# A fixed VectorE order over two row blocks, output terms per step, and a hinted branch in a top-p attention loop

## The chip, the cores and the metric

The kernel runs on one core of one Trainium2 chip. The metric is the device time of one execution in microseconds; lower is better. Each run is repeated, and each study run is timed beside runs of the kernel before on the same chip.

Names: PE is TensorE, PEld its weight load, DVE is VectorE, ACT is ScalarE, POOL is GpSimd. "L589" is line 589 of that kernel's own file, so the same work has different line numbers in different kernels. The granted clock is the share of its full speed at which PE was let run, as the trace recorded it. A branch hint is an instruction that marks a branch as likely to be taken.

## The reference

A graph attention layer over 4096 nodes with 256 features makes `x1`. A second layer takes the layer norm and a relu of it, spreads it over the graph, and does two steps of top-p attention. Only the second layer's attention matters here:

```python
def _top_p_attention(X, W1, W2, W3):
    q = X @ W1.T @ W2.T
    k = X @ W3.T
    logits = q @ k.T / TAU
    probs = jax.nn.softmax(logits, axis=-1)
    idx = jnp.argsort(-probs, axis=-1)
    sp = jnp.take_along_axis(probs, idx, axis=-1)
    cs = jnp.cumsum(sp, axis=-1)
    keep_sorted = cs - sp < TOP_P
    ...  # mask: keep_sorted, back in the order of the columns
    A = probs * mask
    return A / jnp.maximum(A.sum(-1, keepdims=True), 1e-12)
...
for n in range(STEPS):
    A = _top_p_attention(Xa, W1, W2, W3)
    Xf = R @ Xf
    Xa = A @ Xa
    Z = Z + Xf @ U1[n].T + Xa @ U2[n].T
h = X + Z
...  # layer norm of h, times ln_g, plus ln_b; the caller adds x1
```

The attention matrix of 4096 x 4096 is worked in 32 row blocks of 128 rows, in each of the two steps.

## The kernel before

A block passes through these pieces. The threshold of each row is found without sorting: three probes, each of which sums the entries under a guess, then the largest 48 entries under the last guess are sorted.

```python
def second_probe(r):                 # DVE 128x4096, then some 20 small POOL operations give the third guess c3
    nc.vector.scalar_tensor_tensor(big, r.e, r.c2, r.e, ALU.is_le, ALU.mult, accum_out=L)
    ...
def candidates(r):                   # DVE: third probe, maxima of 16 segments, sort, threshold r.t, flags
    nc.vector.scalar_tensor_tensor(big, r.e, r.c3, r.e, ALU.is_le, ALU.mult, accum_out=L)
    ...
    nc.vector.tensor_scalar(flags[:, 1:], after, r.t, flags[:, :1], ALU.is_equal, ALU.max)
    r.count = ps2.tile([P, 512], F32, name="mm")
    nc.tensor.matmul(r.count[:1, :2], ones[:, :1], flags, start=True, stop=True)   # PE counts the flagged rows

def masked(r):
    nc.vector.tensor_copy(cnt, r.count[:1, :2])
    with tc.If(nc.values_load(cnt[:, 1:], **dve) > 0, ...):    # rare: ties, or the threshold not among the 48
        with tc.If(nc.values_load(cnt[:, :1], **dve) > 0):
            searched(r.e, r.z, r.t, big)                       # bisection, over 31 probes: a long piece of program
        untied(r.e, r.z, r.t, big)
    nc.vector.scalar_tensor_tensor(r.e, r.e, r.t, r.e, ALU.is_ge, ALU.mult, accum_out=kept)   # "the mask"
    nc.vector.reciprocal(scale, kept)

def attend(e, scale, cur, dst):      # PE: 8 groups of four transposes and four accumulations; ACT copies between
    ...
def finish(b, xa2):                  # step two only: four output terms on PE, then the layer norm on DVE
    ...

for b in range(NB):
    r = begun.pop(b)
    if b + 2 < NB:
        begun[b + 2] = first_probe(kT, qT, nm, sg, c1, b + 2)   # PE logits, ACT exponentials and sign passes
    candidates(r)
    if b + 1 < NB:
        second_probe(begun[b + 1])
    if b + 2 < NB:
        first_step(begun[b + 2])                                # POOL: second guess c2
    scale = masked(r)
    attend(r.e, scale, cur, xa)
    if n == 0:
        nc.scalar.dma_start(xa_d[b], xa)
    else:
        finish(b, xa)
```

The order of instructions on each engine is set ahead of time by a scheduler that works from program order and estimates; only the dependencies are the programmer's.

## Time and profile before

| | before |
|---|---|
| time, median of 3 runs | 4451.24 us (4449.61 to 4453.26) |
| span of the profiled run | 4455.6 us |
| mask to mask, step one (mean of 31 intervals) | 31.79 us |
| mask to mask, step two | 41.47 us |
| last mask of step one to first of step two | 179.0 us |

The time from the start of one block's mask to that of the next is the measure used throughout: the two loops are 62 such intervals, and what is saved in one is saved 31 times. The prediction shows the lines of this profile.

### The profile page before, as it was taken

Reading aid. Unit: us, or ns where it says so; the run is one execution under the profiler, and the core shown is the slowest. Engines: PE = TensorE matmul, PEld = TensorE weight load, DVE = VectorE, ACT = ScalarE, POOL = GpSimd, SP = SyncE. Lnnn points to the kernel's source line nnn. Section 1 sums busy time; section 2 is a strip of 40 time slices with the busy share of each in tenths; the row PEclk is TensorE's granted clock in tenths of the full one; section 3 lists DMA queues with packets and bytes.
Section 4 is the critical chain, followed back from the end, with each engine's and each line's share of the span. In section 5 each row is a group of like instructions: output and inputs, shape, how many; then the busy total and the mean of one; then the engine's idle time right before and its main releaser. Section 6 shows DMA issues by size and latency. Waiting matters only on the chain. (4 is left out here: it accounts for less than half of the span.)

```text
span 4455.6 us, 55548 instructions
## 1 busy us (share of the span) xinstructions
PE 3426.5 (77%) x19239; PEld 2653.2 (60%) x19239; DVE 2882.5 (65%) x5564; ACT 2161.2 (49%) x4250; POOL 1391.9 (31%) x2857
## 2 busy tenths in 40 slices
PE   3598786879459999758888888885677787787787
PEld 1287786868337777526565655663555565555465
DVE  4587887888535544248686877742756667667565
ACT  2476665757211100356665656536344545544543
POOL 2100000000110000136566565613445454445453
PEclk7599898989659999868888888896788788888888
DMA  7416152440238888100000000010000000000000
GB/s 167 152 68 144 60 129 97 106 115 35 83 108 273 276 282 271 61 2 5 6 4 6 5 5 6 5 43 1 10 15 10 15 13 13 15 15 10 15 13 10
DMA packets 175128, 297.34 MB, mean 67 GB/s; under 512 B 15008, under 2 KB 82592, under 8 KB 174752
## 3 DMA queue, kind: packets, MB, share of 16 engines
q1 hardware_dynamic: 114160, 224.30, 15.4%
q0 software_dynamic: 16896, 33.56, 4.3%
q10 hardware_dynamic: 43696, 35.15, 2.4%
q8 instruction: 154, 2.52, 0.2%
q14 instruction: 222, 1.82, 0.1%
HBM read 292.62 MB, written 33.88 MB: 73 GB/s over the span
## 5 line engine op out<-in xcount | busy, mean ns | idle before, releaser
L641 PE MATMUL acc<-X,eT 128*128 128x256 f32 x4096 | 1014.3, 403 | 18.9 <-ACT eT L638 11.7
L641 PEld LDWEIGHTS acc<-X,eT 128*128 128x128 f32 x4096 | 809.4, 203 | 198.6 <-ACT eT L638 87.2
L228 PE MATMUL acc<-ut,m 128*128 128x195 bf16 (+1 forms) x8192 | 761.9, 255 | 174.6 <-DVE m L222 111.7
L228 PEld LDWEIGHTS <-m 128*128 128x128 bf16 x8192 | 730.0, 100 | 206.6 <-DVE m L222 103.0
L219 ACT ACTIVATE g<-sr,d_c 128x1024 bf16<-128x1024 f32 x512 | 560.4, 1153 | 291.0 <-DVE m L223 267.3
L638 ACT COPY eT<-tp 128x512 f32<-128x512 f32 x512 | 283.5, 587 | 832.1 <-PE tp L636 831.6
L636 PE MATMUL tp<-ident,e 128*128 128x128 f32 x2048 | 344.6, 325 | 378.2 <-DVE e L590 378.2
L301 PE MATMUL racc<-hl,ar 128*128 128x512 f32 x2048 | 515.0, 409 | 148.5 <-DVE hl L284 75.0
L636 PEld LDWEIGHTS tp<-ident,e 128*128 128x128 f32 x2048 | 301.9, 170 | 424.3 <-issue 393.4
L301 PEld LDWEIGHTS racc<-hl,ar 128*128 128x128 f32 x2048 | 391.5, 196 | 271.7 <-DVE hl L284 92.3
L342 PE MATMUL mm<-kT,qT 64*128 64x512 f32 x1024 | 468.1, 719 | 98.0 <-ACT e L461 82.9
L506 POOL TENSOR_TENSOR sums<-sums 128x8 f32<-128x8 f32 (+1 forms) x128 | 215.6, 1684 | 787.9 <-ACT void L498 782.9
L461 ACT ACTIVATE e<-mm,nm 128x512 f32<-128x512 f32 x512 | 346.2, 684 | 183.1 <-PE mm L342 166.5
L590 DVE SCALAR_TENSOR_TENSOR e<-e,t 128x4096 f32<-128x4096 f32 x64 | 287.0, 4484 | 164.1 <-issue 112.5
L222 DVE TENSOR_TENSOR m<-g,ax 128x2048 bf16<-128x2048 bf16 x256 | 313.1, 1223 | 76.5 <-issue 54.8
L342 PEld LDWEIGHTS mm<-kT,qT 64*128 64x128 f32 x1024 | 150.7, 205 | 320.8 <-ACT e L461 254.0
L554 DVE MAX8 cand<-big 128x8 f32<-128x256 f32 x1024 | 340.8, 410 | 0.1
L519 DVE SCALAR_TENSOR_TENSOR big<-e,lowered 128x4096 f32<-128x4096 f32 x64 | 286.9, 4483 | 60.8 <-POOL lowered L476 60.7
L547 DVE SCALAR_TENSOR_TENSOR big<-e,lowered 128x4096 f32<-128x4096 f32 x64 | 286.7, 4480 | 38.1 <-POOL lowered L476 38.1
L223 DVE TENSOR_TENSOR m<-g,ax 128x2048 bf16<-128x2048 bf16 x256 | 311.2, 1216 | 0.0
L496 ACT ACTIVATE void<-e,c 128x1024 uint8<-128x1024 f32 x256 | 293.3, 1146 | 2.2
L297 DVE CAST ar<-at 128x1024 fp32r<-128x1024 f32 x256 | 176.1, 691 | 181.0 <-DMA at<-in_adj_t_dram 149.5
(195 smaller groups left out, 3852.3 us busy)
## 6 DMA issues: line engine op xcount, KB each, us to landing
at<-in_adj_t_dram SPq DMA_DIRECT2D x256, 512.0 KB, 4.7
ut<-uv_d SPq DMA_DIRECT2D x64, 784.0 KB, 7.0
ax<-in_adj_t_dram POOLq DMA_DIRECT2D x32, 1024.0 KB, 9.5
uv_d<-parts ACTq DMA_DIRECT2D x128, 98.0 KB, 1.9
xb<-in_x_dram SPq DMA_DIRECT2D x64, 128.0 KB, 2.1
sr<-s_d SPq DMA_DIRECT2D x16, 512.0 KB, 3.7
x<-x_d SPq DMA_DIRECT2D x64, 128.0 KB, 2.3
xf_d<-xf ACTq DMA_DIRECT2D x64, 128.0 KB, 4.0
```

What stands on the lines that cost most here:

```text
L219: nc.scalar.activation(g[:, c, :], sr, AF.Sign, bias=d_c[:, h, j0 + c:j0 + c + 1])
L222: nc.vector.tensor_tensor(m[0], g, a, ALU.is_equal)
L223: nc.vector.tensor_tensor(m[1], g, a, ALU.is_lt)
L228: nc.tensor.matmul(acc[i][:, t, :cols], m[t][:, c, ts(i, P)], ut[:, j, t, :cols], start=(j == 0 and t == 0), stop=(j == NB - 1 and t == 1))
L301: nc.tensor.matmul(acc[i].rearrange("p s d -> p (s d)"), ar[:, c, ts(i, P)], hl[hop][:, j].rearrange("p s d -> p (s d)"), start=(j == 0), ...
L342: nc.tensor.matmul(pm, qT[ts(c % 2, DA), ts(b, P)], kT[ts(c % 2, DA), ts(c // 2, 512)], start=True, stop=True)
L461: nc.scalar.activation(e[:, ds(c % 2 * N // 2 + c // 2 * 512, 512)], pm, AF.Exp, bias=nm[:, b:b + 1], accum_out=sums[:, c // 2, c % 2:c % ...
L496: nc.scalar.activation(void, r.e[:, ts(q, N // 4)], AF.Relu, bias=r.c1, scale=-1.0, accum_out=sums[:, q, 2:3])
L554: nc.vector.max(cand[:, s, :], big[:, ts(s, N // SEG)])
L590: nc.vector.scalar_tensor_tensor(r.e, r.e, r.t, r.e, ALU.is_ge, ALU.mult, accum_out=kept)
L636: nc.tensor.transpose(pt[:, i, :], e[:, ts(4 * g + i, P)], ident)
L641: nc.tensor.matmul(acc, eT[:, i, :], cur[:, j, :], start=(j == 0), stop=(j == NB - 1))
```

## The change

The intent is to keep VectorE busy across the two waits of a block. VectorE's order is fixed by hand over two row blocks, so that the third probe of block b+1 lies between the flags of block b and the use of their count. The output terms are multiplied in each step right after the attention, and what VectorE has to do with them ("closing": an addition in step one, the layer norm in step two) comes one block later, ahead of the next mask. The rare branch is turned round and hinted. First probes run three blocks ahead instead of two.

```diff
-    ps2 = ctx.enter_context(tc.tile_pool(name="ps2b", bufs=3, space=PSUM))
+    ps2 = ctx.enter_context(tc.tile_pool(name="ps2b", bufs=2, space=PSUM))
-    l1e = ctx.enter_context(tc.tile_pool(name="l1e", bufs=4))
+    l1e = ctx.enter_context(tc.tile_pool(name="l1e", bufs=5))
 ... (logits tiles of two banks; ScalarE pieces twice as wide; fewer GpSimd operations)
     def second_probe(r):
         L = col("L")
-        nc.vector.scalar_tensor_tensor(big, r.e, r.c2, r.e, ALU.is_le, ALU.mult, accum_out=L)
+        nc.vector.scalar_tensor_tensor(junk, r.e, r.c2, r.e, ALU.is_le, ALU.mult, accum_out=L)
 ...
+    def third_probe(r):                       # was the head of candidates(r)
+        r.L = col("L3")
+        nc.vector.scalar_tensor_tensor(big, r.e, r.c3, r.e, ALU.is_le, ALU.mult, accum_out=r.L)
 ...
-    def masked(r):
+    def masked(r, label):
         cnt = small.tile([1, 2], I32, name="cnt", bufs=2)
         nc.vector.tensor_copy(cnt, r.count[:1, :2])
-        with tc.If(nc.values_load(cnt[:, 1:], **dve) > 0, preferred_fallthrough_block=False):
-            with tc.If(nc.values_load(cnt[:, :1], **dve) > 0):
-                searched(r.e, r.z, r.t, big)
-            untied(r.e, r.z, r.t, big)
+        with tc.If(nc.values_load(cnt[:, 1:], **dve) == 0, label=label, preferred_fallthrough_block=False) as none:
+            pass
+        with none.Else():
+            with tc.If(nc.values_load(cnt[:, :1], **dve) > 0):
+                searched(r.e, r.z, r.t, junk)
+            untied(r.e, r.z, r.t, junk)
 ...
-    def finish(b, xa2):
-        ... (four parts transposed and multiplied here, then the layer norm, for step two alone)
+    def contribute(n, r, xf, xa):
+        parts = [transposed(rows, ps2, t, f"zT{i}") for i, t in enumerate((xf, xa))]
+        for i, t in enumerate(parts):
+            for k in range(KC):
+                nc.tensor.matmul(r.acc[:, 1, :], t[:, k, :], u_s[2 * n + i][:, k, :], start=(i == 0 and k == 0),
+                                 stop=(i == len(parts) - 1 and k == KC - 1))
+
+    def finish(n, b, r):
+        if n + 1 < STEPS:
+            nc.vector.tensor_add(r.part, r.acc[:, 1, :], X[:, b, :])
+            nc.sync.dma_start(z_d[b], r.part)
+        else:
+            nc.gpsimd.tensor_tensor(r.x1, r.x1, ln_b_r, ALU.add)
+            hb = rows.tile([P, D], F32, name="hb", bufs=1)
+            nc.vector.tensor_add(hb, r.acc[:, 1, :], r.part)
+            normalized(hb, hb)
+            nc.vector.tensor_mul(hb, hb, ln_g_r)
+            nc.vector.tensor_add(hb, hb, r.x1)
+            nc.sync.dma_start(out[ts(b, P), :], hb)
 ...
-        for b in range(NB):
-            ... (the loop shown above)
+        with tc.manual_schedule(engines={ET.DVE}):
+            second_probe(begun[0])
+            third_probe(begun[0])
+            last = None
+            for b in range(NB):
+                r = begun.pop(b)
+                label = f"usual{n}_{b}"
+                tc.mark_branch_hint_location(label, "LikelyTaken", engines=[ET.DVE])
+                if b + 1 < NB:
+                    second_probe(begun[b + 1])
+                candidates(r)
+                if b + 1 < NB:
+                    third_probe(begun[b + 1])
+                if b + 2 < NB:
+                    first_step(begun[b + 2])
+                if last:
+                    finish(n, b - 1, last)
+                masked(r, label)
+                pair = attend(n, b, r, cur)
+                if b + 3 < NB:
+                    begun[b + 3] = first_probe(kT, qT, nm, sg, c1, b + 3)
+                contribute(n, r, *pair)
+                last = r
+            finish(n, NB - 1, last)
```

## The prediction

> **What bounds the kernel now.** I read the page first: 4455.6 us, and no engine above 77%, so no engine's sum sets the time. Then busy time by stage, to find the stretches that the change touches: the attention loop runs from 1965 us to the end, in two steps of 32 row blocks. In both, PE (about 0.82 busy), DVE (0.75 and 0.67) and ACT leave gaps at once, so the loop is bound by a chain that goes from engine to engine. The columns are stretch, length, PE, PEld, DVE, ACT, POOL busy, PE clock, DMA share, GB/s:
> ```profile
> 2350.00:2550.00 200.00, 165.06 (x689) 118.28 (x689) 149.66 (x321) 124.07 (x258) 117.59 (x228) 0.87 0.02 5
> 2226.20:2230.60 4.40, 0.00 (x0) 0.00 (x0) 4.40 (x3) 3.35 (x6) 0.97 (x1) 0.50 0.00 2
> 3700.00:4000.00 300.00, 241.59 (x1031) 174.25 (x1029) 199.64 (x474) 149.64 (x331) 140.40 (x315) 0.84 0.05 14
> ```
> The list of waits over 3300 to 4400 us (step two; total us, times, longest) gives the chain: DVE waits for PE twice per block, PE waits for DVE once.
> ```profile
> PE tp L636 <- DVE e L590: 205.2, 27, 8.9
> DVE hb L657 <- PE mm L654: 144.4, 26, 6.2
> DVE cnt L583 <- PE mm L578: 103.2, 25, 4.2
> ```
> The timeline of DVE shows one block of step one: after the flags it waits 5.51 us for their count, which PE does in its own order, then 4.06 us with nothing shown (the branch), then masks. I read the end of the flags, the cast and the mask:
> ```profile
> 2216.17 0.27 DVE L576 TENSOR_SCALAR flags<-after,t,flags 128x1 f32<-128x1 f32 x1
> 2221.95 0.15 DVE L583 CAST cnt<-mm 1x2 int32<-1x2 f32 x1 [5.51 <-PE mm L578]
> 2226.16 4.48 DVE L590 SCALAR_TENSOR_TENSOR e<-e,t 128x4096 f32<-128x4096 f32 x1 [4.06 <-issue]
> 2257.77 4.48 DVE L590 SCALAR_TENSOR_TENSOR e<-e,t 128x4096 f32<-128x4096 f32 x1 [1.54 <-DVEq L585]
> ```
> PE in the same block: the count stands late, some logits of a later block are pulled ahead, then it idles 5.73 us for the mask:
> ```profile
> 2221.72 0.19 PE L578 MATMUL mm<-flags,ones 128*1 128x2 f32 x2
> 2222.01 1.26 PE L342 MATMUL mm<-kT,qT 64*128 64x512 f32 x4
> 2223.95 1.12 PE L342 MATMUL mm<-kT,qT 64*128 64x512 f32 x2 [0.67 <-ACT e L461]
> 2230.80 2.79 PE L636 MATMUL tp<-ident,e 128*128 128x128 f32 x12 [5.73 <-DVE e L590]
> ```
> In step two the output layer norm sits between flags and branch, before the count:
> ```profile
> 3752.73 0.42 DVE L657 TENSOR_TENSOR hb<-mm,xin 128x256 f32<-128x256 f32 x1 [5.59 <-PE mm L654]
> 3755.03 0.41 DVE L125 TENSOR_SCALAR hb<-hb,mv,rs 128x256 f32<-128x256 f32 x1 [0.87 <-POOL rs L124]
> 3761.73 0.15 DVE L583 CAST cnt<-mm 1x2 int32<-1x2 f32 x1 [4.17 <-PE mm L578]
> 3763.45 4.48 DVE L590 SCALAR_TENSOR_TENSOR e<-e,t 128x4096 f32<-128x4096 f32 x1 [1.57 <-DVEq L585]
> ```
> A block, mask to mask. Step one: 24.41 us of DVE work without a gap (2226.16 to 2250.57), 5.51 wait, 0.15 cast, 1.54 branch: 31.6. Its masks run from 1968.9 to 2954.3, so the mean is 985.4 / 31 = 31.8. Step two: 24.69 work, 5.59 wait, 4.83 for the layer norms, 4.17 wait, 0.15 cast, 1.57 branch: 41.0; its masks run from 3133.3 to 4419.0, mean 1285.7 / 31 = 41.5. The rest (1965 us of earlier layers, some 179 us between the two runs of masks, some 36 after) is 2180 us.
>
> **What the Trainium skill says.** "TensorE: Matmul & The Clock Gate", section "What's actually happening": the array runs at half clock after an idle window of about 3.4 us and recovers after as much work. The trace agrees: clock 0.50 while PE waits for the mask, and the first 24 accumulation records then take 6.85 us where two later groups of 16 take 3.72 each. "Runtime: NRT & Kernel Launch", section "Instruction fetch mechanics": a taken branch whose target lies outside the fetched window stalls. The trace agrees in kind: 33 gaps ahead of the mask near 1.55 us, 29 near 112.5 / 29 = 3.9 us. "SBUF — State Buffer", section "Who interferes with whom": a DVE instruction with two SBUF inputs shuts out a GpSimd one that reads SBUF. The trace agrees: one POOL 128x1 operation takes 4.62 us beside a 4.49 us probe.
> ```profile
> 3737.48 4.63 POOL L536 TENSOR_SCALAR up<-up,lowered,sg 128x1 f32<-128x1 f32 x1
> ```
>
> **The change, part by part.**
> (1) DVE's order becomes: second probe of b+1, candidates of b, third probe of b+1, closing of b-1, branch and mask of b. Nothing of the 24.41 us is removed; but between flags(b) and the cast now lies the third probe, 4.48 us, which formerly came after the mask. A wait like the 5.51 in step one would shrink to about 1.0.
> (2) Closing one block later. The 5.59 us wait for the output matmuls of the same block disappears, because block b-1 has had a whole block's time. The layer norm of the input rows goes (its result X is added in step one): 0.41 + 0.41 + 0.15 of DVE. Step two keeps add 0.42, statistics 0.43 + 0.19, scaling 0.41, two row operations 0.84: 2.29 us, and the 0.87 wait for POOL's power; the third row addition moves to POOL. Step one gains one addition, 0.42.
> (3) Branch hinted, its bounds check dropped: mean gap (112.5 + 51.4) / 64 = 2.56 us; I take 1.3, the short gap less about 0.2 for the check's two register records. Worth about 1.2 us.
> (4) PE. From the trace at clock 1.0: two groups of four transposes and eight accumulations recur every 4.61 us, so a block's eight take 18.4. Sixteen logits records at 0.39 (3.11 for 8): 6.2. Output terms: four transposes 0.44, eight records of 0.2325 (3.72 / 16): 2.3; they were in step two only, for four parts, and are now half in each step. With the count 0.2: 27.1 us per block in either step.
> (5) ACT: exponentials and sign passes in pieces twice as wide. The fixed cost saved is about 0.1 per piece, 1 us of about 19 per block; ACT is under the others and this is not on the path.
> (6) PSUM: logits buffers 3 to 2 (each two banks), transpose buffers 3 to 2. The projections ahead of each step use the same buffers one bank at a time: their 8 groups and 32 moments passes (some 45 and 18 us now) lose overlap. I allow 1 us per group and 0.13 per pass, 12 us, and 3 more for the further probe ahead of the first mask: an estimate of 15 us per step, 30 in all.
>
> Sums if all waits vanish. Step one: DVE 24.4 + 0.4 + 0.15 + 1.3 = 26.3, PE 27.1: PE bounds. Step two: DVE 24.4 + 2.3 + 0.9 + 0.15 + 1.3 = 29.1: DVE bounds. Floor: 4451 - 31 x (31.8 - 27.1) - 31 x (41.5 - 29.1) + 30 = 4451 - 146 - 384 + 30 = 3951.
>
> I do not take the floor. The engines other than DVE are still ordered ahead of time, by program order and estimated readiness. I put 29.5 for step one and 30.7 for step two: 2.4 and 1.6 us above the floor for count, ACT pieces now 2 us long ahead of a transpose's copy, and POOL. Savings 31 x 2.3 = 71 and 31 x 10.8 = 335. 4451 - 71 - 335 + 30 = 4075; I shade this to 4050, because DVE's waits may shrink further where PE never idles long enough to lose its clock (the cold start costs the 6.85 against 5.6 us above, 1.3 us a block, and I have not taken it off the allowance).
>
> **Rivals.**
> (A) The count keeps a late place on PE: behind attention 18.4, logits 6.2 and output terms 2.3. Then a block is 27.1 + cast 0.15 + branch 1.3 + mask 4.5 + about 0.4 of signals = 33.5 in both steps. For it: it is how both steps run now, and in the program text the count comes after those three. Against: the trace shows logits pulled ahead into PE's idle time, which takes them out from ahead of the next count. Time: 4451 + 53 - 248 + 30 = 4286.
> (B) The second probe needs the first step of POOL sooner than before: it now opens the block, formerly it came some 10 us in, and even so waited 0.28 us in step two. Logits after attention would put it at 18.4 + 6.2 + 1.2 + 8.4 (sign passes) + 4.8 (POOL) = 39 us after the mask two blocks back; with the 29 of DVE work that follow, 68 per two blocks, 34 each, again near 4290. Against: a first probe is three blocks ahead now and five buffers let it start before attention.
> (C) All waits vanish: 3951, or a little under if the prologue loses nothing.
> (D) Reload of a PSUM bank: the count takes a transpose bank from its matmul to the cast, some 5 us, leaving one. A transpose group and copy (0.45 + 0.59) fit inside eight accumulations (1.86), so this costs only when ACT is in a long pass: 1 us or so, inside my allowance.
>
> **Range and chances.** C and A or B bracket it: 3951 and 4290. Most weight lies between, nearer C: 4050, with 3940 to 4190 for 8 in 10. Even A and B leave 3.7%, since step two's 5.59 us wait goes in any case: faster by over 2% 0.96, within 2% 0.03, slower 0.01.
>
> **What would show it.** Right: mask to mask 28 to 31 us in both steps, the count's wait on DVE under 1 us, PE clock over 0.95 in the loop, gaps ahead of the mask all near 1.3 us. A: cast waits of 3 us or more for the count, PE idle some 5 us ahead of the first transposes. B: the second probe waiting for POOL at the start of the block. If the gaps ahead of the mask still split in two kinds, the hint does nothing. If the stretch from the last mask of step one to the first of step two (179 us) grows by more than 40, the banks cost more than I allowed.

## More of the kernel before

One view is added here, the list of waits over 2100 to 2900 us (inside step one) with total us, times and longest: in step one too, the count and the branch were VectorE's two waits.

```profile
DVE cnt L583 <- PE mm L578: 119.8, 24, 5.7
...
DVE e L590 <- issue: 46.2, 12, 4.1
```

## The result, and the profile after

The changed kernel took 4381.38 us (median of 4 runs, 4367.66 to 4390.72) against 4450.42 us for the kernel before in the same rounds (4443.78 to 4453.26): a ratio of 0.9845 with a 95% interval of 0.9816 to 0.9873, so within 2%. Ratios here are the mean time of one kernel's runs over the mean of the other's runs of the same rounds, so they are not quite the ratio of the medians quoted. The outputs were correct.

| | before | after | predicted |
|---|---|---|---|
| mask to mask, step one | 31.79 | 32.63 | 29.5 |
| mask to mask, step two | 41.47 | 37.23 | 30.7 |
| last mask of step one to first of step two | 179.0 | 198.9 | about 194 |
| time | 4450.42 | 4381.38 | 4050 |

Over 31 intervals each, step one lost 26 us, step two gained 131 us, and the stretch between lost 20: 85 us in all, where the two profiled spans differ by 90 (4455.6 and 4365.9). So the whole result is in the loops, and almost the whole of the shortfall too.

Busy time by stage of the changed kernel, columns as in the prediction. VectorE is no busier in step one than before (148.83 of 200 us against 149.66), though it has about the same work to do; PE's clock is a little higher.

```profile
2350.00:2550.00 200.00, 173.11 (x766) 126.22 (x766) 148.83 (x324) 109.50 (x163) 61.08 (x198) 0.91 0.05 14
3700.00:4000.00 300.00, 231.53 (x1008) 169.70 (x1008) 215.67 (x473) 145.48 (x217) 97.21 (x288) 0.86 0.05 15
```

The lists of waits, first over 2100 to 2900 us (step one), then over 3300 to 4400 us (step two). The wait for the count is gone from both; in its place stands a wait of the closing's addition, 4.9 us a block in either step (116.6 / 24 and 131.6 / 27). The profile names no releaser for it ("issue").

```profile
DVE part L671 <- issue: 116.6, 24, 6.3
...
DVE e L589 <- DVEq L582: 58.7, 24, 3.7
```

```profile
PE tp L651 <- DVE e L589: 224.2, 28, 12.0
...
DVE hb L676 <- issue: 131.6, 27, 5.3
```

The timeline gives the releaser. First VectorE in one block of step one, from the mask to the next: the third probe ends at 2347.41, the closing's addition starts 5.08 us later, the cast of the count follows at once, then 3.67 us pass at the branch.

```profile
2322.43 4.49 DVE L589 SCALAR_TENSOR_TENSOR e<-e,t 128x4096 f32<-128x4096 f32 x1 [3.57 <-DVEq L582]
...
2347.33 0.08 DVE L541 DVE_READ_ACCUMULATOR big<-e,lowered 128x1 f32 x1
2352.49 0.42 DVE L671 TENSOR_TENSOR part<-acc,X 128x256 f32<-128x256 f32 x1 [5.08 <-issue]
2352.83 0.14 DVE L580 CAST cnt<-tp 1x2 int32<-1x2 f32 x1
2356.64 4.49 DVE L589 SCALAR_TENSOR_TENSOR e<-e,t 128x4096 f32<-128x4096 f32 x1 [3.67 <-DVEq L582]
```

Then PE in the same block. It has waited 4.01 us for the mask, so the attention starts on a slow clock (granted 0.50; 5.69 us for sixteen accumulation records, two for each matmul, 3.72 later), ends at 2349.02, and the eight records of output terms end at 2352.39, 0.1 us before the addition starts. Only then comes the count, with most of a later block's logits behind it.

```profile
2326.98 1.97 PE L651 MATMUL tp<-ident,e 128*128 128x128 f32 x8 [4.01 <-DVE e L589]
2328.78 5.69 PE L656 MATMUL acc<-X,eT 128*128 128x256 f32 x16
...
2345.30 3.72 PE L656 MATMUL acc<-X,eT 128*128 128x256 f32 x16 [0.29 <-ACT eT L653]
...
2350.50 1.89 PE L666 MATMUL acc<-u,zT 128*128 128x256 f32 x8
2352.32 0.19 PE L575 MATMUL tp<-flags,ones 128*1 128x2 f32 x2
2352.44 1.98 PE L346 MATMUL mm<-kT,qT 64*128 64x512 f32 x6
```

This is the whole loop: the mask of block b-1 ends at 2326.92, its output terms are there 25.5 us later, and VectorE, whose work between is 20.5 us, needs them before it may mask block b. "One block later" is later in the program, but between the same two masks.

Step two closes the same way, with the layer norm behind the wait (3.4 us from the addition to the cast) and before the branch:

```profile
3735.47 4.70 DVE L589 SCALAR_TENSOR_TENSOR e<-e,t 128x4096 f32<-128x4096 f32 x1 [3.90 <-DVEq L582]
...
3765.73 0.42 DVE L676 TENSOR_TENSOR hb<-acc,part 128x256 f32<-128x256 f32 x1 [4.91 <-issue]
...
3769.10 0.14 DVE L580 CAST cnt<-tp 1x2 int32<-1x2 f32 x1
3772.77 4.72 DVE L589 SCALAR_TENSOR_TENSOR e<-e,t 128x4096 f32<-128x4096 f32 x1 [3.53 <-DVEq L582]
```

Last, the masks as one group (busy time, mean ns, idle time before them): the gap at the branch, from VectorE's own sequencer (DVEq), came to 191.6 us for 64 masks where it had been 164.1. It is 2.99 us in the mean: 48 gaps of over 2.4 us, called long from here on, most near 3.6, and 16 short ones near 1.2. The packed trace also has the records of VectorE's sequencer, which the views leave out. They show where a long gap is long: from the end of the cast to the branch instruction it is 0.42 us in both kinds, from the branch instruction to the mask 3.17 us in the long ones and 0.77 in the short (means of 48 and 16). So loading the count into a register is not what differs; the time is lost between the branch and the next work.

```profile
L589 DVE SCALAR_TENSOR_TENSOR e<-e,t 128x4096 f32<-128x4096 f32 x64 | 293.7, 4590 | 191.6 <-DVEq L582 191.6
```

### The profile page after: what moved, and what is told of

Its sections match the earlier page's. It is cut to its first block, busy times and chain, and to the rows that moved or that the text cites. A ratio compares the mean times of both kernels' runs of the same rounds, so it can differ in the third digit from the quotient of the medians.

```text
span 4365.9 us, 54054 instructions
## 1 busy us (share of the span) xinstructions
PE 3344.7 (77%) x19239; PEld 2602.7 (60%) x19239; DVE 2888.0 (66%) x5468; ACT 2020.8 (46%) x3194; POOL 876.6 (20%) x2505
## 5 line engine op out<-in xcount | busy, mean ns | idle before, releaser
L656 PE MATMUL acc<-X,eT 128*128 128x256 f32 x4096 | 1060.2, 417 | 62.8 <-ACT eT L653 62.8
L651 PE MATMUL tp<-ident,e 128*128 128x128 f32 x2048 | 314.9, 305 | 375.6 <-DVE e L589 375.6
L651 PEld LDWEIGHTS tp<-ident,e 128*128 128x128 f32 x2048 | 272.4, 158 | 443.2 <-DVE e L589 332.6
L480 ACT ACTIVATE void<-e,c 128x2048 int8<-128x2048 f32 x256 | 513.1, 2004 | 5.6
L589 DVE SCALAR_TENSOR_TENSOR e<-e,t 128x4096 f32<-128x4096 f32 x64 | 293.7, 4590 | 191.6 <-DVEq L582 191.6
L346 PE MATMUL mm<-kT,qT 64*128 64x512 f32 x1024 | 362.5, 699 | 65.7 <-ACT e L475 55.2
L475 ACT ACTIVATE e<-mm,nm 128x1024 f32<-128x1024 f32 x256 | 284.1, 1118 | 147.7 <-PE mm L346 147.4
L515 DVE SCALAR_TENSOR_TENSOR junk<-e,lowered 128x4096 uint8<-128x4096 f32 x64 | 286.5, 4477 | 54.6 <-POOL lowered L498 54.6
L541 DVE SCALAR_TENSOR_TENSOR big<-e,lowered 128x4096 f32<-128x4096 f32 x64 | 286.7, 4480 | 32.5 <-POOL lowered L498 31.5
L346 PEld LDWEIGHTS mm<-kT,qT 64*128 64x128 f32 x1024 | 104.6, 201 | 239.3 <-ACT e L475 188.7
L312 ACT ACTIVATE xf<-xf,rinv 128x256 f32<-128x256 f32 x64 | 32.6, 510 | 418.1 <-DVE xf L311 314.0
```

The costliest lines, as they stand in the source:

```text
L346: nc.tensor.matmul(pm[:, h, :], qT[ts(h, DA), ts(b, P)], kT[ts(h, DA), ts(c, 512)], start=True, stop=True)
L480: nc.scalar.activation(void, e[:, ts(h, N // 2)], f, bias=r.c1, scale=-1.0, accum_out=r.sums[:, h, 2 + i:3 + i])
L651: nc.tensor.transpose(pt[:, i, :], r.e[:, ts(4 * g + i, P)], ident)
L656: nc.tensor.matmul(r.acc[:, 0, :], eT[:, i, :], cur[:, j, :], start=(j == 0), stop=(j == NB - 1))
```

## The experiments

Three suspects: the closing ahead of the mask, the count's place in PE's order, and the gap at the branch. Every kernel is the changed one plus the edit shown. All gave correct outputs on these inputs. Two of them (e5 and e13s) leave out the bisection of the rare branch and would be wrong where a row needs it; they are tests, not versions. The rare branch is never entered on these inputs (the changed kernel's trace has nothing on its lines), so a gap is only the way past it.

### e1: closing behind the mask

```diff
-                if last:
-                    finish(n, b - 1, last)
                 masked(r, label)
+                if last:
+                    finish(n, b - 1, last)
```

> Edit: the closing of block b-1 moves from ahead of the branch of block b to behind its mask, on DVE alone. Theory (PE round trip): the closing and the count both stand behind attention, logits and output terms of b-1 in PE's order, so the wait of about 5 us only moves from the closing's addition to the cast; step one stays at 32.6 us a block within 0.6, step two loses just the layer norm (3.4 us) from the path, 37.2 to about 33.9, and the time is about 4380 - 31 x 3.4 = 4275. Rival (the closing alone is the mistake): the wait goes in both steps, 5 us a block, and the time is about 4380 - 31 x 5 - 31 x 8.4 = 3965.

Measured: 4239.47 us, ratio 0.9529 (0.9513 to 0.9545); step one 32.07 us a block, step two 33.28. That is near the theory (4275 us, 32.6 and 33.9) and far from the rival (3965). The closing's wait is gone, and step two gained 4 us a block. Step one gained only 0.6: VectorE now waits for the count instead, 4.2 us a block, in the first line below. In the second, PE does that count behind its output terms, as before.

```profile
2325.32 0.15 DVE L580 CAST cnt<-tp 1x2 int32<-1x2 f32 x1 [5.01 <-PE tp L575]
```

```profile
2325.09 0.19 PE L575 MATMUL tp<-flags,ones 128*1 128x2 f32 x2
```

So two waits of about the same length lay one under the other. In step two the layer norm now behind the mask fills most of the second.

### e3: as e1, and the count at high priority

```diff
+        with tc.high_priority():
             nc.tensor.matmul(r.count[:1, :2], ones[:, :1], flags, start=True, stop=True)
```

> Edit: as e1_finish_after, and the count's matmul gets first claim in PE's order, which puts it ahead of the output terms but still behind the attention of b-1. Theory (PE round trip): the count comes about 1.7 to 2.3 us earlier after the mask, and each block gets shorter by just that, about 110 us in all against e1_finish_after: about 4165. Rival (branch fetch is what eats the gain, the count is not on the path): no change against e1_finish_after beyond 20 us.

Measured: 4247.65 us, 0.9547 (0.9531 to 0.9563); step one 31.95, step two 33.69. No gain over e1. The scheduler put the count ahead of the output terms, but also moved six logits records ahead of the attention. Over 25 blocks of step one, the count ended 25.1 us after the mask in the mean, in e1 25.0; so the edit did not bring it earlier. A priority was not enough to test the count's place; e13 and e19 do it by hand.

### e4: no hints

```diff
-                tc.mark_branch_hint_location(label, "LikelyTaken", engines=[ET.DVE])
```

> Edit: the line that marks the branch hint is taken out. In the built program all 64 hints stand at the very top of DVE's stream, so I expect no effect: gaps ahead of the mask still in two kinds, near 1.2 and 3.5 us, mean about 3.0, the time within 15 us of the changed kernel (4381). Rival (the hints do something, good or bad): the mean gap moves by over 0.5 us and the time by over 30 us.

Measured: 4320.27 us, 0.9713 (0.9692 to 0.9734). The expectation of no effect fell: the hints cost about 61 us. With them away, 28 of 64 gaps are long instead of 48. Nearly all of that is step two, with 31 of 32 long before and 14 now; step one had 17 and has 14. The idle time before the masks, from the view of the mask's line in this kernel (191.6 in the kernel with hints):

```profile
  DVEq L582: 143.5, 64
```

The 48 us saved there are most of the 61.

### e5: the bisection left out of the rare branch

```diff
-            with tc.If(nc.values_load(cnt[:, :1], **dve) > 0):
-                searched(r.e, r.z, r.t, junk)
```

> Edit: the search inside the rare branch is left out (128 of its about 140 instructions; it is never entered with these inputs, so the result should stay right, but with other inputs it would be wrong). Theory (the long gap is instruction fetch over the skipped body): nearly all gaps are 1.2 us, so 1.8 us a block less, about 64 x 1.8 = 115 us: about 4270. Rival (the gap is the register load and branch itself): gaps and time as in the changed kernel.

Measured: 4215.73 us, 0.9471 (0.9455 to 0.9487), hints in place; one long gap, mean gap 0.85 us. With a short piece of program to jump over, all but one of the long gaps vanish. What was taken out is never executed, so its presence alone in the program costs time. Whether by its length or by where it puts the branch's target, this run doesn't tell.

### e7: no hints, and 64 fills at the top of VectorE's stream

```diff
 ... (as e4)
+    fill = const.tile([P, 1], F32, name="fill")
+    for k in range(64):
+        nc.vector.memset(fill, 0.0)
```

> Edit: no hints, and 64 tiny fills of a scratch column at the top of DVE's stream in their place. e4_no_hint was 61 us faster than the changed kernel and had 28 long gaps against 48. Theory (the hints at the top do nothing but shift every later DVE instruction by 64 places against the blocks in which instructions are fetched): the gaps are again 48 long of 64 in the same pattern and the time is 4381 within 12. Rival (the hints do harm as hints): as e4_no_hint, 28 long gaps, about 4320.

Measured: 4315.22 us, 0.9687 (0.9671 to 0.9703); 28 long gaps, mean 2.23 us, as in e4 (4320.27). All 64 hints of the changed kernel run at the top of VectorE's stream (0.76 to 5.63 us in its trace), since the hand order doesn't bind them, and this run put as many other instructions there. The idea that the hints hurt by pushing the stream along by 64 places fell.

### e10: each hint pinned just ahead of its own branch

```diff
-                tc.mark_branch_hint_location(label, "LikelyTaken", engines=[ET.DVE])
 ...
                 candidates(r)
+                likely = nc.values_load(zero_i, engines=[ET.DVE], ...)     # a register read pins it here
+                tc.mark_branch_hint_location(label, likely, engines=[ET.DVE])
```

> Edit: each hint takes its verdict from a register that DVE loads (always 0) just ahead of the third probe, which holds the hint there, some 10 us before its branch. Theory (the hint works where it stands near its branch): nearly no long gaps, mean 1.2 us, about 115 us off the changed kernel: about 4270. Rival (the hint does not help a jump of this kind): long gaps remain in about half of the blocks or more, 4320 to 4390.

Measured: 4384.43 us, 0.9838 (0.9817 to 0.9859); 47 long gaps, mean 3.02 us. The same as the changed kernel, though the hints now run 5 to 17 us ahead of their branches by the trace: a hint so near its branch is no better than one at the top. That idea fell too.

### e14: hints for step two alone

```diff
+                if n == 1:
                     tc.mark_branch_hint_location(label, "LikelyTaken", engines=[ET.DVE])
```

> Edit: hints for the 32 branches of step two only, still placed by the scheduler at the top. Theory (a hint changes its own branch's layout or fetch, wherever the hint itself stands): step one shows the pattern of the kernel without hints (about 13 long of 32), step two that of the hinted one (31 long). Rival (hints at the top act once, by delay or by shift): both steps look alike, as with or as without.

Measured in one run, state unknown: 4375.48 us; 14 of 32 gaps are long in step one, as without hints, and 27 of 32 in step two. So the harm goes with the hints of step two, wherever they stand. How they do it, and why those of step one hardly matter (17 long with them), stays open.

### e15: no hints, and fills in the rare branch that are never executed

```diff
 ... (as e4)
             untied(r.e, r.z, r.t, junk)
+            pads((18, 13)[r.n])             # so many memsets, inside the rare branch
 ...
+        pads((65, 36)[n])                   # and so many once ahead of each step
         kT, qT, nm, sg, c1 = projections(cur)
```

> Edit: the changed kernel without hints, with 18 (step one) and 13 (step two) never executed fills at the end of each rare branch, and 65 and 36 executed ones ahead of the two loops. Without hints long and short gaps come in runs that repeat every 7 blocks in step one and every 9 to 10 in step two. Theory (the gap depends on where the branch and its target lie against blocks of the instruction stream, of 128 places or a multiple): with the stride made a multiple the pattern stands still, all gaps of a step are alike, and the offset chosen for the middle of the short runs makes them short: 0 to 4 long, about 4240. If the offset is wrong, all long in a step, up to 4390, which would still show placement. Rival (data or timing decides): the mixture stays, about 28 long, 4318.

Measured: 4254.15 us, 0.9544 (0.9528 to 0.956); 9 long gaps, all in step one, mean 1.52 us, where the expectation had 0 to 4. The branch jumps over more instructions than in e4, yet 19 more gaps are short, so it isn't the length as such; what the fills change is where branch and target lie in VectorE's instruction stream. The theory's 128 places were not tested against another number. The idle time before the masks:

```profile
  DVEq L583: 97.4, 64
```

It is 46 us less than in e4, for 66 us of time. Where the rest comes from was not tested.

### e8: PE's order fixed by hand as well, first probe three blocks ahead

PE's order per block becomes: attention of b, count of b+1, logits of b+3 with the output terms of b after their first piece. The count gets a place in the accumulator's bank, and the attention's transposes run two groups ahead of its accumulations. The closing lies behind the mask.

```diff
-        with tc.manual_schedule(engines={ET.DVE}):
+        with tc.manual_schedule(engines={ET.DVE, ET.PE}):
 ...
+                masked(r, label)
+                if last:
+                    finish(n, b - 1, last)
+                pair = attend(n, b, r, cur)
+                if b + 1 < NB:
+                    ahead(b + 1)            # second probe b+2, candidates and count b+1, third probe b+2
+                if b + 3 < NB:
+                    begun[b + 3] = first_probe(kT, qT, nm, sg, c1, b + 3, lambda: contribute(n, r, *pair))
+                    first_step(begun[b + 3])
```

> Edit: PE's order fixed by hand too: attention, then the count of the next block, then logits and output terms; the closing behind the mask as in e1; the count kept in the accumulator's bank rather than in a transpose buffer. Theory (PE round trip): the count now comes about 19 us after the mask, ahead of the end of the third probe, so DVE waits under 0.5 us for it and PE's idle time shrinks; a block is 28 to 29.5 us in step one and 30 to 31.5 in step two, 4060 to 4120. Rival (PE's own speed with two transpose buffers is the bound): 31 us or more in both steps with PE busy throughout, 4190 or more.

Measured: 4902.55 us, 1.1004 (1.0985 to 1.1022), some 44 us a block. The expectation fell: VectorE's second probe waits 17.50 us for GpSimd's guess.

```profile
2332.77 4.48 DVE L517 SCALAR_TENSOR_TENSOR junk<-e,lowered 128x4096 uint8<-128x4096 f32 x1 [17.50 <-POOL lowered L500]
```

The logits of b+3 now stand behind the count of b+1, and the second probe of b+3 opens the very next interval. Between them lie the exponentials, four sign passes of 2 us each with their accumulators, and the guess on GpSimd. That is a ring, count to logits to sign passes to guess to probe to flags to the next count, and a block takes as long as the ring. It is rival B of the prediction in kind, with some 44 us a block instead of its 34.

### e11: as e8, with pinned hints

> Edit: e8_pe_order with the pinned hints of e10. If both theories hold, gaps are 1.2 us, step one comes to PE's own 27.5 to 28.5 us and step two to 28.5 to 30: 3960 to 4050. If the hint does not help, as e8_pe_order.

The edits are those of e8 and e10 together. Measured: 4912.88 us, 1.1025 (1.1007 to 1.1044). The ring hides the gap; this run tells nothing of hints.

### e13: as e8, first probe four blocks ahead, no hints

```diff
 ... (on e8; the hints out as in e4, four first probes ahead of the loop)
-                if b + 3 < NB:
-                    begun[b + 3] = first_probe(kT, qT, nm, sg, c1, b + 3, lambda: contribute(n, r, *pair))
-                    first_step(begun[b + 3])
+                if b + 3 < NB:
+                    first_step(begun[b + 3])
+                if b + 4 < NB:
+                    begun[b + 4] = first_probe(kT, qT, nm, sg, c1, b + 4, lambda: contribute(n, r, *pair))
                 else:
                     contribute(n, r, *pair)
```

> Edit: e8's hand order of PE without hints, with the first probe begun four blocks ahead instead of three, so that the logits on PE behind the count serve a block one later. In e8 the count was early, but DVE's second probe waited 17.5 us in step one for a first probe whose logits stood behind the count. Theory (a ring: count, logits, sign passes, POOL step, second probe, flags, count; one more block of distance breaks it): the second probe's wait is gone, the cast's too, a block is about 28 us in step one and 29 to 30.5 in step two with 2.2 us mean gaps: 3990 to 4070. Rival (PE's strict order and the transposes' copies behind 2 us ACT passes bound it): 31 us or more a block, 4180 or more.

Measured: 4042.0 us, 0.9064 (0.9047 to 0.908); step one 28.18, step two 30.56. It is 861 us under e8; two things were changed, but the hints were worth only 61 (e4), and VectorE's wait for GpSimd's guess is gone. One block more of distance opens the ring, and the hand order is worth what e8 was meant to show. PE's granted clock is 1.00 and 0.95 in windows inside steps one and two.

### e13s: as e13, bisection left out

> Edit: e13_pe_ahead with the search of the rare branch left out as in e5 (not for use: wrong where the branch is taken). If DVE bounds step two, its gap of 0.85 in place of 2.2 us gives 1.4 us a block there; if PE bounds step one (27.3), little there: 3930 to 4020. If both are PE's, no change against e13_pe_ahead.

The edit is that of e5 on e13. Measured: 3966.61 us, 0.89 (0.8884 to 0.8915); no long gap, mean 0.78 us; step one 27.79, step two 29.07. This is a test of the sums: the prediction's floor had 27.1, 29.1 and 3951 us, with a gap of 1.3 us.

### e16: e13 with padding in the rare branch

```diff
 ... (as e15, on e13; 20 and 12 fills in the rare branches, 65 and 100 ahead of the steps)
```

> The kernel with the hand order on TensorE too and the first probe four blocks ahead (4042.0 us), with fills that are never executed in the rare branches so that their targets move in VectorE's stream. It computes the right result on every input, rare branch included. If the gap of VectorE before the mask is a matter of the place of the branch and its target alone, nearly all 64 gaps are short (28 were long, by some 2.4 us each): up to 67 us less, 3975 to 4010 us. If the gap is hidden in this order, or the remedies do not add up, 4030 to 4050 us. If the padding falls badly for this stream, up to 64 long gaps and 4090 us.

Measured: 3984.89 us, 0.8945 (0.8932 to 0.8958); step one 27.84, step two 29.54, no long gap. Idle time before the masks:

```profile
  DVEq L586: 76.1, 64
```

That is 1.19 us each, and 57 us of time against e13 for 28 gaps shortened. It keeps the rare branch whole and is faster than both kernels. The padding is tuned to this one instruction stream: any edit of VectorE's program may undo it.

### e17: e13 with the closing put back ahead of the mask

```diff
+                if last:
+                    finish(n, b - 1, last)
                 masked(r, label)
-                if last:
-                    finish(n, b - 1, last)
```

> The same kernel with hand order on TensorE and the first probe four blocks ahead, but with the closing of the block before put back ahead of the branch and the mask, as the change under study has it. Theory: the closing's place hurt only because the output terms came late on TensorE; here they are ready, so VectorE waits under 1 us for them, step one takes 28.2 to 28.8 us a block, step two 30.6 to 31.5, 4040 to 4090 us in all. Rival: closing ahead of the branch costs by itself, because the attention of the interval before bounds it: some 4 to 5 us a block again, about 4300 us.

Measured: 4295.76 us, 0.9636 (0.9622 to 0.9651); step one 31.74, step two 35.36. The theory fell and the rival held. VectorE waits 4.4 us a block for the output terms (111.1 us in 25 times over 2100 to 2900 us). First VectorE, then PE, in one block of step one:

```profile
2296.47 4.49 DVE L592 SCALAR_TENSOR_TENSOR e<-e,t 128x4096 f32<-128x4096 f32 x1 [1.19 <-DVEq L585]
...
2325.62 0.42 DVE L681 TENSOR_TENSOR part<-acc,X 128x256 f32<-128x256 f32 x1 [4.19 <-issue]
```

```profile
2301.02 1.09 PE L654 MATMUL tp<-ident,e 128*128 128x128 f32 x8 [2.80 <-DVE e L592]
2302.35 3.65 PE L664 MATMUL acc<-X,eT 128*128 128x256 f32 x8 [0.24 <-ACT eT L656]
...
2323.53 1.99 PE L676 MATMUL acc<-u,zT 128*128 128x256 f32 x8 [1.03 <-ACT zT L132]
```

Here PE is ordered as well as in e13, and still the mask ends at 2300.96 and the output terms at 2325.52, 24.6 us later, with 20.5 us of VectorE's work to hide them. Behind the mask, VectorE has the cast, the gap and the next mask as well, some 6 us more (0.15 + 1.2 + 4.5), and the wait is gone. So the closing's place costs by itself.

### e18: e1 without hints

> The change with the closing behind the mask and without the hints, TensorE's order left to the tool: the missing corner of a square of four kernels without hints (closing ahead and TensorE ordered by the tool 4320 us, closing ahead and TensorE by hand 4296, closing behind and TensorE by hand 4042). If the two remedies simply add: 4320 - (4296 - 4042) = 4066 us. Theory: they do not add, because here the count stands behind the output terms on TensorE, so VectorE's wait goes over to the count in step one (about 4 us, 31.5 to 32.0 us a block) and mostly goes in step two (32.5 to 33.2): 4170 to 4200 us.

The edits are those of e1 and e4 together. Measured: 4200.97 us, 0.9423 (0.9403 to 0.9443); step one 31.81, step two 32.16. VectorE's wait for the count is 4.1 us a block in step one (102.8 / 25). This is the fourth corner of a square of kernels without hints:

| | PE ordered by the scheduler | PE ordered by hand, as in e13 |
|---|---|---|
| closing ahead of the mask | 4320.27 (e4) | 4295.76 (e17) |
| closing behind the mask | 4200.97 (e18) | 4042.0 (e13) |

Moving the closing alone gains 119 us, ordering PE alone 25, both together 278. If they added, the fourth corner would stand near 4176. It lies 134 us below, since each wait lies under the other. The right column holds all that e8 and e13 changed on PE, the fourth block ahead and the accumulator's bank too; e19 tests the count's place alone. (The expectation's own sum, 4066, took e17 for its base instead; the theory's 4170 to 4200 was met within 1 us.)

### e19: e13 with the count behind the logits and the output terms

```diff
-        nc.tensor.matmul(r.count[:1, :2], ones[:, :1], flags, start=True, stop=True)
+        r.do_count = lambda: nc.tensor.matmul(r.count[:1, :2], ones[:, :1], flags, start=True, stop=True)
 ...
                 else:
                     contribute(n, r, *pair)
+                if b + 1 < NB:
+                    begun[b + 1].do_count()
```

> The kernel with the hand order on TensorE and the first probe four blocks ahead (4042.0 us), with one matmul moved: the count of the block goes behind the first probe's logits and the output terms instead of ahead of them. Theory: this place alone is what the hand order on TensorE is worth; the count then ends some 26 to 30 us after the mask before it, VectorE waits 3 to 6 us for it in step one and 1 to 3 us in step two: step one 31.5 to 34, step two 31.5 to 34, 4150 to 4280 us. Rival: the hand order is worth its time for another reason (logits further ahead, spread evenly), and the count's place costs under 1 us a block: 4040 to 4090 us.

Measured: 4369.97 us, 0.9812 (0.9796 to 0.9828); step one 34.71, step two 34.87. The direction was the theory's, the size more than it gave: VectorE waits 7.5 us for the count in step one (172.9 / 23) and 3.8 in step two (64.5 / 17). One matmul of 0.19 us in another place costs 328 us. In the block read, PE ends its attention at 2325.48, the block's logits and output terms follow, and the count starts at 2333.59, when VectorE has been waiting since 2326.66:

```profile
2333.59 0.19 PE L578 MATMUL acc<-flags,ones 128*1 128x2 f32 x2
```

```profile
2333.81 0.15 DVE L583 CAST cnt<-acc 1x2 int32<-1x2 f32 x1 [7.15 <-PE acc L578]
```

All sixteen logits records stand ahead of the count here, only two in e18. Over 25 blocks of step one it ends 28.4 us after the mask here, 25.0 in e18, and 34.71 against 31.81 us a block go with that.

## Why the prediction was wrong, point by point

**The bound.** That the loop is bound by a chain between PE and VectorE, and not by an engine's sum, was right; after the change it was bound the same way.

**Part (2), the closing: the step that failed.** It said that the wait for the output matmuls "disappears, because block b-1 has had a whole block's time". It hadn't. The attention of b-1 begins when its mask ends, and the closing was placed ahead of the mask of b, so both lie between the same two masks: 25.5 us of PE against 20.5 us of VectorE, a wait of 4.9 us a block in each step. The prediction's own numbers could have warned: attention 18.4 and output terms 2.3 make 20.7, and VectorE's work outside the mask is about 20, so nothing was left to spare. They alone would give a wait of under 1 us. The rest is what they left out: in the block shown, the attention took 22.0 us, 2.9 of it because its first two groups ran on the slow clock, and from its end to that of the output terms, with two logits records between, another 3.4. An estimate from these lines without the slow clock, 25.5 - 2.9 = 22.6, is still over 20.5. Moving the closing behind the mask (e1) took the wait away; putting it back into a well ordered kernel (e17) brought it back and cost 254 us against e13. The 0.96 for a gain of over 2%, and the bracket of 3951 to 4290 us, rested on this step as well: rivals A, B and C all take this wait to be gone, so none of them could give 4381. The sizes in that part were right: 3.4 us from the addition to the cast in step two, 3.2 predicted (2.29 + 0.87).

**Part (1), the count.** "A wait like the 5.51 in step one would shrink to about 1.0" failed as well, but was hidden under the closing's wait. The third probe does lie between flags and cast. The count still stands behind attention and output terms on PE, and once the closing is out of the way VectorE waits 4.2 us for it (e1). This is rival A's cause. A gave 33.5 us in both steps; 32.6 and 37.2 were measured, as A too took the closing to be free, while in step two the layer norm came behind the wait. That step one came near A is luck: another wait, of about the same length, bound it. The prediction weighed against A that logits were pulled out from ahead of the count. They were (14 of 16 records come behind it); the output terms were not. The count ahead of them by hand (e13) against behind (e19) is the clearest proof: 4042 and 4370 us.

**Part (3), the branch.** 1.3 us was predicted for every gap; the mean was 2.99. The short gap was sized right (1.2), the belief that the hint makes all gaps short was wrong: with the hints 48 gaps are long, without them 28. That is 61 us of time (e4). That the place in the instruction stream matters is shown by e15 and e16, where fills in the rare branch, which never run, and more ahead of the loops, which do, change the gaps. By what mechanism the hints lengthen those of step two was not settled.

**Part (4) and the floor.** PE's sum of 27.1 us and VectorE's of 29.1 were good: e16 has 27.84 and 29.54, e13s 27.79 and 29.07. The floor of 3951 us is 34 us under e16.

**Part (5), ScalarE.** Mis-sized, but not on the path, as it said. The mean exponential of 512 columns took 0.69 us before and that of 1024 takes 1.12, the sign passes 1.14 and 2.00, so merging two pieces saves about 0.26 us, where 0.1 a piece was put; ScalarE is busy for 17.6 us a block in place of 19.3 (2100 to 2900 us), 1.7 less and not 1.

**Part (6), the stretch between the steps.** It grew by 19.9 us, 15 predicted; of little weight.

**The allowance.** On top of the floor 2.4 and 1.6 us a block were set aside for all that the scheduler might do. The measured excess over the floor is 5.5 (32.63 - 27.1) and 8.1 (37.23 - 29.1). Of the 331 us between 4050 and 4381, the excess over the 29.5 and 30.7 that were put is 97 and 202 us (31 x 3.13 and 31 x 6.53), and 25 are the shading from 4075 to 4050. Rival B, which was treated as a tail, did not occur in the changed kernel but in e8, as soon as the logits stood behind the count with too little distance. Rival D, the reload of a PSUM bank, was not tested by itself.

## What to carry to other kernels

When work is put off "by one block", draw both ends between the masks (or whatever the loop turns on) and compare the engines' times in that one interval: a delay that doesn't cross the turning point hides no more than the other work in that interval. Where an engine's order is fixed by hand, fix that of the engine it waits for as well, short handshakes first and with enough blocks of distance for the longest ring; waits lie on top of one another, so a remedy tried alone can look nearly worthless (25 us) and be worth 159 beside the other. Measure a branch hint before keeping it.

## What the Trainium skill lacked or had wrong

- Branch hints: no page has them. Here 64 hints gave 48 long gaps and a mean of 2.99 us, without them 28 and 2.24 us (e4), wherever the hint stood (e10: 3.02 us).
- "Runtime: NRT & Kernel Launch", section "Instruction fetch mechanics", says that a taken branch with a target outside the fetched window stalls, but gives no time. The gap here is 1.2 us when short and some 3.6 us when long; never executed fills, which move branch and target in the stream, brought the long ones from 28 to 9 (e15) and from 28 to 0 (e16), and the whole difference lies behind the branch instruction (3.17 against 0.77 us). That the fetched window is the cause fits, and no run here shows the fetches themselves.
- "TensorE: Matmul & The Clock Gate", section "What's actually happening", gives an idle window of about 3.4 us, free-running, for the half clock, and doesn't say how idle. In e17, of the 20 waits of PE for the mask listed between 2100 and 2720 us, 14 are only 2.78 to 2.82 us long, and in each of those the transposes that follow still run at full speed (1.09 us for eight records) while the first eight accumulation records, which start 1.3 us after the transposes do, take 3.50 to 3.68 us instead of 1.89. So idle times under 3.4 us did cost the clock here, every time, and the slow stretch came after work had begun again. The trace's record of the granted clock changes at multiples of 3.41 us alone, which agrees with the page, but the window need not be idle throughout: of the 491 at full clock in e17 between 2000 and 4200 us, 62 were followed by the half clock, and in 61 of these PE was busy for up to 49%; in the other 429 it was busy for 53% or more. That share is no rule: in the kernel before (2000 to 4400 us), PE was busy for over half of 42 of the 62 windows ahead of a drop. What is counted stays open.
- "SBUF — State Buffer", section "Who interferes with whom", says that the order of issue decides who blocks whom, without a size for this pair. The changed kernel's trace agrees. In step two GpSimd's new 128x256 addition starts 0.26 to 0.30 us ahead of the mask 28 times: it takes 0.72 or 0.73 us, and the mask 4.70 to 4.75 us instead of 4.49. Twice it starts behind the mask: then the mask takes 4.49 us and the addition 4.95 and 5.01.
